# Second routing of a two-layer graph-attention kernel: one more step ahead of the normed row, the row's copy on another engine, later tables, more bias buffers

## The chip, the cores and the metric

The kernel runs on one core of one Trainium2 chip. The metric is device time in microseconds (us), the median of several executions. TensorE is written PE, its weight loads PEld, VectorE DVE, ScalarE ACT, GpSimd POOL; SP is the engine that issues most transfers.

## The reference

Two layers are computed on 2708 rows `x` of 256 numbers. Each layer is a graph attention, then a mixture of eight experts, both added to `x`.

```
x = x + elu(softmax(mask(q k^T / 16)) v)            # first attention, q, k, v of layernorm(x)
x = x + sum over top 2 of w_e * expert0_e(layernorm(layernorm(x)))
x = x + softmax(mask(s_src_i + s_dst_j)) H          # second attention, H = layernorm(x) W + b
x = x + sum over top 2 of p_e * expert1_e(layernorm(x))
```

An expert is two matrix products with a Gelu between them, 256 to 512 to 256 in the second layer. A router (a product with an 8-column matrix) chooses two experts for every row. All is in float32; the mask is an adjacency matrix of integers. The change touches the second layer's routing and experts.

## The kernel before, in words

**Tiles and stages.** The rows are cut into 22 tiles of 128 (the last has 20), numbered 0 to 21. In time the stages are: first attention (to 526 us), first experts (529 to 868), keys and values of the second attention with its first group of tiles (868 to 943), groups 1 to 4 of the second attention (943 to 1056), second experts (1059 to 1265), and the final sum (to the end).

**The second attention** (`layer1_attention`) takes its tiles in groups of 6, 6, 4, 3 and 3 (`GROUPS`). For each group it runs over the 22 blocks of keys, `k`, and in each block multiplies every tile of the group twice (line 713; line 719 for the last block), so that a block of a group of six has 12 matmuls. The sums stay in PSUM and are copied out by `evict` (line 739), which also adds a routing job for each tile to a `Line`.

**The line and its steps.** A routing job is a Python generator, and each `yield` ends a step. `line.step()` advances all jobs that run, oldest first, and starts a waiting one when `line.gap` steps have passed since the last. It is called once for each block of keys in groups of four or six tiles, once for every second block in groups of three, and twice in each slot of the experts. The gap is three steps in groups 1, 3 and 4 and in the slots, and five in group 2. So the tiles of group 0 are routed while group 1 is multiplied, and so on; the last ones are routed beside the first slots of the experts.

**The steps of one tile**, with names used below:

- `z`: the denominators of the softmax (`over_sum`, lines 244 to 249, DVE).
- statistics: the attention is added to `kept` (line 727), the logits are completed (line 730), and `norm_stats` takes mean and variance (lines 209 to 211) and a power -0.5 on POOL (line 215, `ln_rs`).
- row: `normed` makes the row that the experts read (line 219, DVE, needs the power); POOL writes the token number into two rows (line 956) and copies the first row into the second (line 969; DVE does so once `begun` is set).
- `lg`: the gate logits, the two best experts and the selection `sel` (lines 986 to 1007, DVE).
- the exponential of the two best (line 1009, ACT).
- the counting product on PE (lines 1012 and 1013, need `sel` and `seen`).
- `den`: weights and positions (lines 1016 to 1029, DVE), which end with `to`, the row numbers; `seen` is brought up to date (line 1023); then POOL dispatches the two rows into a DRAM table `disp` by indirect transfers (line 1032).

**Early tables.** When 14 tiles are routed (`early`), `begin` starts a generator beside the line: it calls `place` for the first 20 chunks of rows, each of one expert (a product at line 1053 that needs `seen`, then DVE work over lines 1055 to 1144), and then asks for the rows (line 1204, SP) and weights (line 1189, POOL) of the first three chunks.

**The slots of the second experts** (`slots`). A slot s multiplies one chunk of 128 rows: `up` (line 1260, eight pairs of 128x128, Gelu at line 1268), the transposition of the next chunk (line 1237, copied to `xe` at line 1247), a step of the line, `down` of slot s-1 (line 1276), in whose middle slot s+3's weights and rows are fetched, and another step. `down` adds the bias copy `bias2` on DVE (`y`, line 1282), scales it, and POOL stores the rows (line 1287). `bias2` is copied by ACT at the head of `up` (line 1253). Weights lie in a ring of four buffers; a fetch whose chunk has the same expert as the one four slots before moves no data. After slot 8's first step the remaining chunks are placed by a second call of `place`.

**Order.** PE, ACT, DVE and SP take their instructions in the order of the program text here (`manual_schedule`); POOL's order is chosen by the planner. [...]

Of the kernel before, what the change touches and what calls it, by code (L numbers as in the profile page):

```python
# [9 lines left out]
F32 = mybir.dt.float32  # L10
# [10 lines left out]
P = 128  # L21
N = 2708
D = 256
# [39 lines left out]
AHEAD = 3  # L63
# [6 lines left out]
def adj_ffn_kernel(ctx: ExitStack, tc: tile.TileContext, a: dict, out: bass.AP):  # L70
    nc = tc.nc
# [531 lines left out]
    def layer1_attention(mTs, kept, line, first_masks):  # L603
        with ExitStack() as scope:
# [100 lines left out]
            def attend(ts_, k, accs):  # L705
                if k == GROUP:
                    load_tails(ts_)
                masks = next(masks_of_keys) if k < NT - 1 else None
                for t, acc in zip(ts_, accs):
                    r, j = ROWS[t], t % GROUP  # L710
                    if masks:
                        for i in range(2):
                            nc.tensor.matmul(  # L713
                                acc[:r], masks[t], parts[:, k, i],
                                start=(k == 0 and i == 0), stop=False,
                            )
                        continue
                    keys = slice(j * QUARTER, j * QUARTER + TAIL)
                    nc.tensor.matmul(
                        acc[:r, : VALUES + 1], tails[t // GROUP][keys, :r], e_tail[keys], start=False, stop=True  # L720
                    )
# [14 lines left out]
            def evict(ts_, accs, total):  # L736
                for j, (t, acc) in enumerate(zip(ts_, accs)):
                    raw = rows.tile([P, VALUES + 1], F32, name="raw", bufs=6)
                    (nc.scalar.copy if j % 2 else nc.vector.tensor_copy)(  # L739
                        raw[: ROWS[t]], acc[: ROWS[t], : VALUES + 1]  # L740
                    )
                    line.add(finish(t, raw, total))

            def keys_and_values(ts_, accs):

                nc.scalar.activation(spread_of[:, :1], ident[:, :1], AF.Exp)
                def busy(n):  # L750
                    for _ in range(n):
                        nc.tensor.matmul(  # L752
                            accs[0][:, :D], ident, wfc[:, 0, :D], start=True, stop=True
                        )

                busy(PAUSE)
                next(masks_of_keys)
                stats, xn, xT, e = {}, {}, {}, {}
                for i in range(-3, NT + LAG1 - 1):
                    if i + 3 < NT:  # L760
                        stats[i + 3] = norm_begin(i + 3)
                    if 0 <= i - 1 < NT:
                        add_bias(i - 1)
                    if 0 <= i - 1 < NT - 1:
                        second_part(i - 1, e.pop(i - 1))
                    if 0 <= i + 2 < NT:
                        xn[i + 2] = norm_end(i + 2, *stats.pop(i + 2))
                    if 0 <= i + 1 < NT:
                        xT[i + 1] = columns(i + 1, xn.pop(i + 1))
                        if i < 1:  # L770
                            busy(1 - i)
                    if 0 <= i < NT:
                        e[i] = values(i, xT[i])
                    if 0 <= i - 2 < NT:
                        attend(ts_, i - 2, accs)
                    if 0 <= i < NT:
                        nc.vector.tensor_reduce(
                            sums_of[:, :, i], xT.pop(i)[:, :, : ROWS[i]], AX.X, ALU.add
                        )
# [5 lines left out]
            g0, total, beginning = 0, None, None  # L785
            for g, wide in enumerate(GROUPS):
                if g == 2:

                    assert g0 >= FIRST_MASKS * GROUP
                    first_masks.close()  # L790


                    n = FULL_AFTER[experts1.early]
                    guess = experts1.open(
                        [i * (n // RING) * E // (n + GROUP) for i in range(RING)],
                        lambda: converted_last[0],
                    )
                ts_ = list(range(g0, g0 + wide))
                accs = [ps_acc.tile([P, EVEN], F32, name="acc") for _ in ts_]

                every = 2 if wide < GROUP else 1
                line.gap = NT // wide // every
                if g == 0:
                    with tc.manual_schedule(engines={mybir.EngineType.Pool}):
                        keys_and_values(ts_, accs)
                for k in range(NT if g else 0):
                    if g > 0:
                        if g == 2 and k % GROUP == 0:
                            next(guess, None)
                        attend(ts_, k, accs)  # L810
                        if k % every == 0:
                            line.step()
                    if g > 0 and not experts1.begun and experts1.routed >= experts1.early:
                        beginning = experts1.begin()
                    if beginning:
                        next(beginning, None)
                if g == 0:
                    sums = pool.tile([P, DC], F32, name="sums", bufs=1)
                    nc.vector.tensor_reduce(sums, sums_of, AX.X, ALU.add)
                    total = all_sum(pool, sums, wfc, VALUES, "total1")  # L820
                    nc.vector.tensor_add(
                        logits, logits, bfc_gate.unsqueeze(1).to_broadcast([P, NT, E])
                    )
                evict(ts_, accs, total)
                g0 += wide
# [41 lines left out]
    class Experts:  # L867
# [64 lines left out]
        def route(self, t, x, logits=None):  # L932


            own_norm, xd, disp, seen = self.own_norm, self.xd, self.disp, self.seen
            w_gate, gate_bias = self.w_gate, self.gate_bias
            r = ROWS[t]
            rows2 = [
                routing.tile([P, DROW], F32, name=f"row{j}") if own_norm
                else kept_pool.tile([P, DROW], F32, name=f"row{j}", bufs=6)  # L940
                for j in range(2)
            ]
            mean, once, twice, _ = norm_stats(x[:r], r)
            yield
            if own_norm:
                self.beside_early(nc.sync.dma_start(xd[t * P : t * P + r, :], x[:r]))

# [7 lines left out]
            for j in range(2):  # L955
# [4 lines left out]
                if not own_norm:  # L960
# [5 lines left out]
                        ),  # L966
                        reason="no sooner than the row",
                    )
            (nc.vector if own_norm or self.begun else nc.gpsimd).tensor_copy(
                rows2[1][:r, :D], rows2[0][:r, :D]  # L970
            )
            yield
            lg = small.tile([P, E], F32, name="lg")
            if logits is None:
                gT = routing.tile([P, DC, P], F32, name="gT", bufs=2)
# [173 lines left out]
        def begin(self):  # L1149

            assert self.routed >= self.early
            self.begun = True
            return self.begin_steps()

        def begin_steps(self):
            yield from self.place(0, FULL_AFTER[self.early])
            rows_ = [self.fetch_rows(s) for s in range(AHEAD)]
            self.fetched = [(self.fetch_weights(s), rows_[s]) for s in range(AHEAD)]

        def open(self, likely=None, pace=None):  # L1160

# [67 lines left out]
        def slots(self, two, ps_mm, ps_tp, ps_acc, line):  # L1229
            hidden, own_norm, xd = self.hidden, self.own_norm, self.xd  # L1230
# [18 lines left out]

            def up(w, xe):  # L1250

                bias2 = two.tile([P, D], F32, name="bias2")
                (nc.vector.tensor_copy if own_norm else nc.scalar.copy)(bias2, w[:, b2:b1])
                hT = two.tile([P, hc, P], F32, name="hT")
                for g in range(0, hc, GROUP):
                    ps = ps_mm.tile([P, GROUP, P], F32, name="mm")
                    for i in range(GROUP):
                        f = g + i
                        for c in range(DC):
                            nc.tensor.matmul(  # L1260
                                ps[:, i, :],
                                w[:, c * hidden + f * P : c * hidden + (f + 1) * P],
                                xe[:, c, :],
                                start=(c == 0), stop=(c == DC - 1),
                            )
                    for i in range(GROUP):
                        f = g + i
                        nc.scalar.activation(  # L1268
                            hT[:, f, :], ps[:, i, :], AF.Gelu, bias=w[:, b1 + f : b1 + f + 1]
                        )  # L1270
                return hT, bias2
# [103 lines left out]
    experts1 = Experts(1, 512, packed1, wg, gb_b, False, xd1, disps[1], 14)  # L1375
# [79 lines left out]
```

## Time and profile before

| what | us |
|---|---|
| median of 3 runs (lowest, highest) | 1306.93 (1302.76, 1307.99) |
| profiled execution, its own time | 1296.54 |
| its span, first to last instruction | 1294.8 |
| PE busy | 1204.9 |
| DVE busy | 552.4 |
| ACT busy | 439.1 |
| POOL busy | 424.3 |

Durations come from the profiled execution alone. In a line of the timeline the first number is the start in us from the span's start, the second the duration, and a bracket gives the idle time of the engine before it and what ended it. "issue" there means that the profile shows no releaser. Line numbers are those of the kernel before.

### The profile page before, as it was taken

To read this page: it belongs to the slowest core of one execution; us is meant where nothing else is said; L and a number is where in the kernel's file an instruction comes from. 1 tells how busy PE (TensorE), PEld (TensorE's weight loads), DVE (VectorE), ACT (ScalarE), POOL (GpSimd) and SP (SyncE) were. 2 spreads that over 40 slices of the span, in tenths; PEclk is the share of its full clock that TensorE was granted. 3 is DMA by queue.
4 is the path that set the end of the run, shared out by engine and by line. 5 is a ranking of instruction groups with operands and counts; after the bars stand their busy time and mean duration, and the time that the engine had idled before them with its cause. 6 is when DMAs were issued, how large, how long until landed. Compare 5 with 4: busy or idle time off the path is not lost. (4 is left out here: it accounts for less than half of the span.)

```text
span 1294.8 us, 20983 instructions
## 1 busy us (share of the span) xinstructions
PE 1204.9 (93%) x7136; PEld 972.2 (75%) x7136; DVE 552.4 (43%) x2087; ACT 439.1 (34%) x1286; POOL 424.3 (33%) x553
## 2 busy tenths in 40 slices
PE   7999999999999999999999999999998768899990
PEld 4776666656566675799999999988998757799880
DVE  6623833634625526542212121217767766311114
ACT  3221212212122212433232323325765447444440
POOL 4100110110110113243333333335645557555450
PEclk9999999999999999899999999999999979999995
DMA  8601364996946715356657745432005115544357
GB/s 268 223 1 66 107 179 124 255 239 175 261 112 159 168 62 231 143 170 171 212 160 243 281 121 173 110 99 85 1 26 189 42 58 180 174 137 145 119 180 261
DMA packets 107242, 197.83 MB, mean 153 GB/s; under 512 B 26753, under 2 KB 81718, under 8 KB 100986
## 3 DMA queue, kind: packets, MB, share of 16 engines
q1 hardware_dynamic: 77276, 110.09, 29.8%
q0 software_dynamic: 27040, 83.56, 20.4%
q10 hardware_dynamic: 2814, 2.77, 0.7%
q8 instruction: 59, 0.97, 0.3%
q14 instruction: 53, 0.43, 0.1%
HBM read 263.63 MB, written 66.12 MB: 255 GB/s over the span
## 5 line engine op out<-in xcount | busy, mean ns | idle before, releaser
L1260 PEld LDWEIGHTS mm<-xe,ring 128*128 128x128 f32 x2192 | 268.5, 196 | 28.9 <-ACT xe L1247 15.0
L1260 PE MATMUL mm<-xe,ring 128*128 128x128 f32 x2192 | 277.7, 281 | 12.2 <-ACT xe L1247 8.7
L1276 PE MATMUL acc<-ring,hT 128*128 128x256 f32 x1096 | 267.4, 382 | 3.0 <-ACT hT L1268 3.0
L1268 ACT ACTIVATE hT<-mm,ring 128x128 f32<-128x128 f32 x548 | 156.1, 368 | 255.7 <-issue 181.6
L1276 PEld LDWEIGHTS acc<-ring,hT 128*128 128x128 f32 x1096 | 195.3, 191 | 23.2 <-ACT hT L1268 3.6
L504 PE MATMUL acc<-v,p 128*128 128x257 f32 (+1 forms) x880 | 209.7, 390 | 0.0
L447 PE MATMUL s<-g,xnT 128*128 128x512 f32 x420 | 205.6, 604 | 4.1 <-DVE mT L459 4.1
L1282 DVE TENSOR_TENSOR y<-acc,bias 128x256 f32<-128x256 f32 x92 | 39.0, 424 | 368.5 <-PE acc L1276 365.6
L504 PEld LDWEIGHTS acc<-v,p 128*128 128x128 f32 (+1 forms) x880 | 153.7, 191 | 18.3 <-issue 0.8
L1189 POOL DMA_INDIRECT ring<-L_ffn_packed,weight_row x98 | 102.9, 1050 | 195.4 <-issue 153.2
L1032 POOL DMA_INDIRECT disp<-row,to x88 | 88.1, 1001 | 145.7 <-DVE to L1029 57.8
L215 POOL TENSOR_TENSOR ln_rs<-ln_rs,minus_half 128x2 f32<-128x2 f32 x88 | 66.4, 755 | 200.7 <-DVE ln_rs L211 183.4
L713 PE MATMUL acc<-parts,m 128*128 128x266 f32 x924 | 129.2, 297 | 1.8 <-DVE raw L739 1.1
L459 DVE TENSOR_SCALAR mT<-s 128x512 fp8e4<-128x512 f32 x105 | 72.0, 686 | 130.4 <-ACT p L458 130.3
L713 PEld LDWEIGHTS acc<-parts,m 128*128 128x128 f32 x924 | 119.5, 190 | 9.2 <-issue 3.3
L458 ACT ACTIVATE p<-s 128x512 f32<-128x512 f32 x105 | 62.3, 594 | 165.3 <-PE s L453 165.1
L447 PEld LDWEIGHTS s<-g,xnT 128*128 128x128 f32 x420 | 75.1, 191 | 50.1 <-issue 41.6
L1294 POOL DMA_INDIRECT xd<-y,xg x45 | 70.9, 1577 | 80.4 <-issue 36.4
L453 PEld LDWEIGHTS <-apart 128*128 128x128 fp8e4 x420 | 32.7, 99 | 61.2 <-issue 61.2
L685 ACT CAST m<-mT 128x512 fp32r<-128x512 fp8e4 (+4 forms) x168 | 70.6, 473 | 14.1 <-PE acc L713 11.8
L334 DVE TENSOR_SCALAR apart<-adj 128x677 fp8e4<-128x677 int32 x80 | 40.9, 514 | 53.3 <-DMA adj<-in_adj_dram 52.7
L1287 POOL DMA_INDIRECT xd<-y,xg x47 | 47.3, 1006 | 21.1 <-PE tp L1237 8.5
(227 smaller groups left out, 1158.6 us busy)
## 6 DMA issues: line engine op xcount, KB each, us to landing
adj<-in_adj_dram SPq DMA_DIRECT2D x84, 338.5 KB
L_ffn_packed<-in_L_ffn_W_dram SPq DMA_DIRECT2D x16, 1024.0 KB
xg<-disp SPq DMA_DIRECT2D x98, 129.0 KB
L_ffn_packed<-in_L_ffn_W_dram SPq DMA_DIRECT2D x16, 512.0 KB
neighbours<-mT SPq DMA_DIRECT2D x5, 1408.0 KB
mT<-neighbours SPq DMA_DIRECT2D x5, 1408.0 KB
xin<-in_x_dram SPq DMA_DIRECT2D x42, 128.0 KB
ring<-L_ffn_packed SPq DMA_DIRECT2D x4, 1154.0 KB
```

The source lines that it names most:

```text
L215: nc.gpsimd.tensor_tensor(rs[:r, 1], rs[:r, 0], minus_half[:r], ALU.pow)
L447: nc.tensor.matmul(ps[:kr, :nb], xnT[:, c, k0 : k0 + kr], g[:, c, :nb], start=(c == 0), stop=False,)
L459: nc.vector.tensor_scalar(mT[:kr, k, :], ps[:kr, :nb], -BIG / 2, None, ALU.is_gt, saturate=False,)
L504: nc.tensor.matmul(accs[j][:r], p[keys, q0 : q0 + r], v[keys, k, :], start=(k == 0), stop=(k == NT - 1),)
L685: nc.scalar.copy(m[:, : q1 - q0], mTs[b][:, k, q0 - b * BN : q1 - b * BN])
L713: nc.tensor.matmul(acc[:r], masks[t], parts[:, k, i], start=(k == 0 and i == 0), stop=False,)
L1032: nc.gpsimd.indirect_dma_start(disp[:], bass.IndirectOffsetOnAxis(ap=to[:r, j : j + 1], axis=0), rows2[j][:r], None,)
L1189: nc.gpsimd.indirect_dma_start(w, None, packed[:], bass.IndirectOffsetOnAxis(ap=self.weight_row[:, s : s + 1], axis=0), bounds_check=E * P ...
L1260: nc.tensor.matmul(ps[:, i, :], w[:, c * hidden + f * P : c * hidden + (f + 1) * P], xe[:, c, :], start=(c == 0), stop=(c == DC - 1),)
L1268: nc.scalar.activation(hT[:, f, :], ps[:, i, :], AF.Gelu, bias=w[:, b1 + f : b1 + f + 1])
L1276: nc.tensor.matmul(ps, hT[:, f, :], w[:, w2 + f * D : w2 + (f + 1) * D], start=(f == 0), stop=(f == hc - 1),)
L1294: start = nc.gpsimd.indirect_dma_start(xd[:], at, y, None, bounds_check=N - 1, oob_is_err=False, compute_op=ALU.add)
```

## The change

It has four parts, all in the second layer. A tile's routing gets an empty step between its statistics and its normed row. The copy of the first row into the second moves one step later and from POOL to ACT (to DVE, as before, once `begun` is set). The generator that `begin` returns has one more step ahead of it, sets `begun` only then, and asks for one chunk's weights in a step, where it asked for three in one. The bias copy in the slots has four buffers, where it had two. The first layer takes the same code with `own_norm` set: its row and its bias are as they were, and its generator of early tables is run through at one place.

```diff
-                    if g > 0 and not experts1.begun and experts1.routed >= experts1.early:
+                    if g > 0 and not beginning and experts1.routed >= experts1.early:
                         beginning = experts1.begin()
...
             mean, once, twice, _ = norm_stats(x[:r], r)
             yield
+            if not own_norm:
+
+                yield
...
-            (nc.vector if own_norm or self.begun else nc.gpsimd).tensor_copy(
-                rows2[1][:r, :D], rows2[0][:r, :D]
-            )
+            if own_norm:
+                nc.vector.tensor_copy(rows2[1][:r, :D], rows2[0][:r, :D])
             yield
+            if not own_norm:
+                (nc.vector.tensor_copy if self.begun else nc.scalar.copy)(
+                    rows2[1][:r, :D], rows2[0][:r, :D]
+                )
             lg = small.tile([P, E], F32, name="lg")
...
         def begin(self):
 
             assert self.routed >= self.early
+            return self.begin_steps()
+
+        def begin_steps(self):
+            yield
             self.begun = True
-            return self.begin_steps()
-
-        def begin_steps(self):
             yield from self.place(0, FULL_AFTER[self.early])
             rows_ = [self.fetch_rows(s) for s in range(AHEAD)]
-            self.fetched = [(self.fetch_weights(s), rows_[s]) for s in range(AHEAD)]
+            self.fetched = []
+            for s in range(AHEAD):
+                self.fetched.append((self.fetch_weights(s), rows_[s]))
+                yield
...
-                bias2 = two.tile([P, D], F32, name="bias2")
+                bias2 = two.tile([P, D], F32, name="bias2", bufs=2 if own_norm else 4)
```

More of the change, by code (lines that the diff above doesn't have):

```diff
@@ L1151, in begin @@
             assert self.routed >= self.early
-            self.begun = True
             return self.begin_steps()
         def begin_steps(self):
+            yield
+            self.begun = True
             yield from self.place(0, FULL_AFTER[self.early])
             rows_ = [self.fetch_rows(s) for s in range(AHEAD)]
-            self.fetched = [(self.fetch_weights(s), rows_[s]) for s in range(AHEAD)]
+            self.fetched = []
+            for s in range(AHEAD):
+                self.fetched.append((self.fetch_weights(s), rows_[s]))
+                yield
         def open(self, likely=None, pace=None):
```

## The prediction

> **What bounds the kernel now.** I read the busy times by stage first, then the waits of the second routing, then the timeline of VectorE and GpSimd around one tile. Only 944 to 1130 us is touched: all edited lines but the generator of `begin` ask for `not own_norm`, and in the first experts that generator is run through at once. The stages are groups 1 to 4 of the second attention and the first twelve slots of the second experts. The columns are PE, PEld, DVE, ACT and POOL busy with counts, the granted clock, DMA share and GB/s:
>
> ```profile
> 945.20:978.70 33.50, 32.31 (x266) 31.80 (x266) 26.28 (x140) 19.32 (x52) 17.11 (x33) 1.00 0.09 33
> 980.00:1007.60 27.60, 22.55 (x185) 21.80 (x185) 17.62 (x96) 13.11 (x36) 14.22 (x29) 1.00 0.61 218
> 1007.60:1027.80 20.20, 19.01 (x141) 18.02 (x138) 15.06 (x79) 10.40 (x32) 10.79 (x19) 0.92 0.10 35
> 1027.80:1059.50 31.70, 20.03 (x144) 16.91 (x141) 24.54 (x133) 11.59 (x50) 18.92 (x29) 0.90 0.21 63
> 1059.50:1072.00 12.50, 10.73 (x49) 9.74 (x50) 3.57 (x18) 7.92 (x18) 2.33 (x6) 0.58 0.07 22
> ```
>
> The reader is to see PE almost full in group 1 (first row) and then losing ground: 5 of 27.6 us in group 2, and 11.7 of 31.7 in group 4 with the wait for its eviction (fourth row). The fifth row, slots 0 and 1, runs at clock 0.58. The waits of the routing (line, releaser, total us, times, longest) name what is late:
>
> ```profile
> DVE row L219 <- POOL ln_rs L215: 29.1, 21, 3.5
> ...
> ACT bias L1253 <- DVE y L1282: 10.6, 5, 4.3
> ```
>
> Line 219 is the normed row; it sits in VectorE's queue and waits for GpSimd's power. One tile of group 3, in the timeline of all engines:
>
> ```profile
> 1022.53 0.41 DVE L219 TENSOR_SCALAR row<-kept,ln_mv,ln_rs 128x256 f32<-128x256 f32 x1 [0.84 <-POOL ln_rs L215]
> ...
> 1023.78 0.17 DVE L1029 TENSOR_REDUCE to<-hot 128x2 int32<-128x16 f32 x1
> ...
> 1027.38 0.72 POOL L215 TENSOR_TENSOR ln_rs<-ln_rs,minus_half 128x2 f32<-128x2 f32 x1 [0.18 <-DVE ln_rs L211]
> ...
> 1028.13 0.41 DVE L219 TENSOR_SCALAR row<-kept,ln_mv,ln_rs 128x256 f32<-128x256 f32 x1 [0.84 <-POOL ln_rs L215]
> ```
>
> From row to row is 5.60 us: 4.76 of VectorE work and 0.84 in which VectorE stands at the row for the power. The work by its starts in this timeline: row 0.33, `den` to `to` 1.01 (1.09 until `to` is ready), `lg` to `sel` 1.02 (1.11 until ready), `z` 0.97, statistics 1.43. Twelve attention matmuls a step (36 a tile, 0.129 us each) give PE 4.64 us a tile, so PE is released by VectorE (`sel`, line 1007) here. In group 2 the loop is longer:
>
> ```profile
> 987.00 0.17 DVE L1029 TENSOR_REDUCE to<-hot 128x2 int32<-128x16 f32 x1
> ...
> 987.95 1.04 POOL L1032 DMA_INDIRECT disp<-row,to  x1 [2.88 <-issue]
> ...
> 991.07 0.41 DVE L219 TENSOR_SCALAR row<-kept,ln_mv,ln_rs 128x256 f32<-128x256 f32 x1 [2.56 <-POOL ln_rs L215]
> ```
>
> `to` (ready at 987.17) releases the two dispatches at 987.95; only behind them does GpSimd take the next tile's power (990.29), and the row comes 3.9 us after `to`. PE needs 5.2 us a tile there, the loop takes 7.1 (row at 991.07, next at 998.18). At the end of group 4:
>
> ```profile
> 1054.80 0.17 PE L1012 MATMUL misc<-sel,before 128*128 128x8 bf16 x1 [3.52 <-DVE sel L1007]
> ...
> 1059.61 0.66 PE L1237 MATMUL tp<-ident,xg 128*128 128x128 f32 x2 [3.43 <-issue]
> ```
>
> PE waits 3.5 us for a row stalled behind GpSimd, and 3.4 for the last accumulators, whose VectorE copy (1058.76 to 1059.51) stands behind the same queue.
>
> [...] The trace agrees: it grants half clock for 3.4 us from 1008.5 and from 1035.8, and for 13.7 us from 1056.3, four such pieces, each after a stretch of these waits. [...]
>
> **The change, part by part.**
>
> *One step more ahead of the row.* A tile takes eight steps for seven. In group 2 a tile starts each fifth step. Before, the next tile's statistics were issued just behind `to` in the same step, so its power queued behind the two dispatches. Now they are issued a step ahead of `to`, the power goes ahead of the dispatches, and the row comes two steps (2.1 us) after the statistics. The loop becomes PE's own 5.2 us; the waits 1.22, 1.88 and 1.88 go: 5.0 us. Late next is PE itself.
>
> In groups 1, 3 and 4 a tile starts each third step, and there the step separates nothing: the added step is one in which VectorE has nothing else, so the row still follows its statistics directly. Worse, `z` of the next tile (0.97 us) now lies between row and `to`, and the power stays behind the dispatches. The new loop is row to `to` 0.33 + 0.97 + 1.09 = 2.39, `to` to dispatch 0.79, two dispatches 2.33, power and row 0.77: **6.28 us** a tile for 5.60. In group 1 the tiles 2 to 5 pay it; the first two have no dispatches ahead. With tile 1's row at 953.6, tile 2's comes 6.65 later at 960.3 and tile 4's at 972.8; its `sel` is 0.33 + 0.97 + 1.01 + 1.11 later, 976.3. PE is there at 974.7, waits, and ends group 1 at 976.3 + 4.64 + 1.1 = 982.1 for 979.8: 2.3 us lost. Group 2 then costs 176 matmuls x 0.1295 + 1.0 = 23.8: it ends at 1005.9 for 1007.6. Group 3 takes 132 x 0.129 = 17.0, plus 0.9 for its last wait and the tails: 1023.8 for 1027.8. The half clock at 1008.5 (1.7 us) should go with group 2's waits. In group 4 PE needs 17.6 us, and VectorE is behind: the rows of tiles 12 and 13 come at 1019.2 and 1025.5; `sel` of 13 is 0.33 + 0.97 + 0.77 (eviction) + 1.01 + 1.11 later, 1029.7, and PE is there at 1027.7: 2.0. Tile 14's row is 3.89 after tile 12's `to`, 1032.6, tile 13's `seen` 2.0 later and 0.2 more to PE; PE comes to line 1053 at 1032.1: 2.7. Then VectorE has one `lg`, one statistics, the whole table and the next `den` and `lg`, 10.9 us, until tile 15's `sel` at 1045.5; PE is there at 1041.8: 3.7. Two statistics, a row with its stall, `z`, `den`, a copy, `lg` and the eviction, 8.5 us, end at 1054.0; PE is there at 1050.3: 3.7. So the eviction ends 30 us after 1023.8, for 31.7: slots begin about 1053.8 for 1059.6, **6 us** earlier.
>
> *Row copy by ScalarE.* Fifteen 0.39 us copies (line 969) leave GpSimd, whose wait hides them in the loop above, so no gain. ScalarE takes 0.41 for one (its 128x256 copy, line 1253) with 14 us idle in the 33.5 of group 1: no cost while the row is ready a step before; its cover is the row's lead of 3.4 us over `sel`. Queued behind it are the mask casts, made two steps of keys ahead. If it were late, the second dispatch waits for it (rival D).
>
> *Early tables a step later, one gather per step.* Three gathers (1.05 us each, line 1189), three row loads on SP, the table's VectorE chain of about 4.6 us: none added. The placing matmul now comes a step of keys behind `seen` (0.8 us): its wait of 2.91 at line 1053 stays at the 2.7 above because VectorE is late itself. The row loads go out at about 1043 and land in 2.2 to 8.8 us; slots begin at 1054. The gathers no longer stand together ahead of a dispatch (3 x 1.35 us at 1044.9 to 1048.9 before the tile-14 pair): tile 16's power is 2.7 us earlier, counted above.
>
> *Four bias buffers.* ScalarE's copy of the bias waits for the `y` of two slots before, which releases its buffer, and Gelu and `xe` are behind it:
>
> ```profile
> 1109.66 0.40 ACT L1253 COPY bias<-ring 128x256 f32<-128x256 f32 x1 [4.31 <-DVE y L1282]
> ```
>
> By this the next matmuls came 1.78 us late. Other such waits in slots 2 to 10: 0.73, 1.60, and 0.9 of one of 2.69; with the 1.8, 5.0 can go. But GpSimd is full there (26.6 busy of 33.75, the rest mostly 0.3 us pieces between DMAs), and real gathers of weights were issued at 1079.1, 1084.5 and 1087.8. In the new order slot 7's comes behind 3 gathers (1.35), 3 stores (1.32), 4 dispatches (1.3), 2 powers (0.9) and 2 index pairs (0.45): 15.9, plus 0.9 to its start and 6.7 to land: 23.5 us after slot 0's down product, for 24.9. Behind slot 9 the 1.8 go. **3 us**, between 0 and 5.0. Slots 0 and 1 I leave at half clock[...].
>
> Sum: 6 + 3 = **9 us**. The profiled execution took 1296.54 (span 1294.8), 0.8% under the median 1306.93; the saving is in the same stages, so I take it off the median: 1298.
>
> **The rivals.** About 0.5% (6.5 us) is what a measurement here can tell from no change. *A, above:* 1298, own range 1291 to 1304. *B, the waits vanish.* If the power no longer stands behind the dispatches in groups 3 and 4, VectorE's 4.76 us a tile is left: 10 tiles x 1.5 = 15 us beyond A's groups at most, of which PE can use about 8, and a clock kept full in slots 0 and 1 gives 5: 1306.9 - 22 = 1285. For it: GpSimd was 10.8 of 20.2 us busy in group 3. Against: [...]the order in them puts the dispatches first. *C, given back.* The clock stays half for two windows more, 2 x 1.7 us, and the slots stay tied to GpSimd's chain of 34 us from slot 0: 9 - 3.4 - 3 = 3 us, 1304. *D, slower.* ScalarE's row copy comes later than 0.79 + 1.34 = 2.1 us after `to`, behind casts that wait for PE, and holds the second dispatch, so the loop of 6.28 grows. At 7.2 us over the 10 tiles of groups with a gap of three the 9 us are gone; at 8 it is 10 x 1.7 - 9 = 8 us slower, 1315. Against: the row is ready a step before. That the change does nothing: if all loops stayed as they are, 1307; the instruction order moved, so only part of C.
>
> **How the numbers follow.** A 0.57 (0.49 of it beyond 6.5 us), B 0.14, C 0.17, D 0.12. Faster 0.63, same 0.25, slower 0.12. The range 1286 to 1309 leaves out D and the far end of B.
>
> **What would show it.** In the timeline after: rows 6.3 us apart in groups 1 and 3, 5.2 in group 2; group 2 without waits for `sel`; line 1053 still waiting over 2 us; slots begun 5 to 7 us earlier; no wait of the bias for `y`. Rows 5.6 or fewer us apart in group 3 make my loop wrong; a second dispatch long after the first makes D right; slots beginning no earlier make the sum wrong.

## The result, and the profile after

The change made the kernel faster. In the comparison beside the kernel before, four runs each, it took 1290.99 us (1287.64 to 1294.16) against 1305.96 (1302.76 to 1307.99): a ratio of 0.9881, with a 95% interval of 0.985 to 0.9912. Measured twice more as a base of the experiments, the same kernel gave 0.9903 [0.9876, 0.9931] and 0.9928 [0.9901, 0.9954]. The mean of the three is 0.990, so about 12 us of 1300 are gained, where 9 were forecast; the first comparison shows 15. The profiled execution took 1287.64 us (span 1285.9), against 1296.54 (1294.8) before. Of these 9 us, 4.5 lie ahead of the second routing (the copy of `total` that opens it comes at 939.59 for 944.10), in instructions that the change leaves alone, so spans are not compared below. What is compared is the stretch from that copy on.

The stages first, in the same columns as before (start and end, length, PE, PEld, DVE, ACT and POOL busy with counts, clock, DMA share, GB/s): groups 1 to 4 and the first slots of the kernel after. Its lines stand lower by the lines added above them: `sel` is line 1013 (1007 before), `to` 1035 (1029), the dispatch 1038 (1032), the table's product 1059 (1053), the transposition 1247 (1237), Gelu 1278 (1268).

```profile
940.70:975.60 34.90, 33.30 (x272) 32.37 (x273) 24.67 (x134) 21.00 (x56) 14.39 (x30) 1.00 0.09 31
975.60:1000.50 24.90, 23.76 (x184) 23.05 (x184) 21.09 (x114) 15.12 (x43) 14.43 (x23) 0.93 0.72 241
1000.50:1017.40 16.90, 16.90 (x145) 16.36 (x141) 13.36 (x74) 11.52 (x35) 8.65 (x15) 1.00 0.11 38
1017.40:1046.40 29.00, 21.66 (x142) 17.78 (x139) 22.91 (x123) 11.87 (x52) 16.56 (x25) 0.86 0.24 70
1046.40:1058.90 12.50, 10.91 (x69) 10.10 (x70) 6.37 (x33) 6.96 (x19) 5.79 (x8) 0.77 0.10 33
```

Against the rows of before, PE is no longer losing ground in group 2 (23.76 of 24.90 us, where it had 22.55 of 27.60) and is never idle in group 3 (16.90 of 16.90). The clock of group 2 is 0.93, for 1.00: a piece of half clock of 3.4 us fell at its start. Group 4 still has 7.3 us of idle PE, for 11.7. The slots start with less half clock: 0.77 for 0.58.

The waits of the same stretch say the same of VectorE (line, releaser, total us, times, longest). PE's wait for a selection before:

```profile
PE misc L1012 <- DVE sel L1007: 12.2, 10, 3.5
```

And the waits after:

```profile
DVE row L219 <- POOL ln_rs L215: 19.8, 15, 2.0
...
PE misc L1018 <- DVE sel L1013: 3.6, 4, 1.4
...
PE misc L1018 <- DVE hot L1006: 1.8, 1, 1.8
```

The row's wait for its power has 15 cases for 21 and a longest of 2.0 us for 3.5, but it is not gone. PE's waits for a selection fall from 12.2 us to 5.4: the 3.6 of the second line, and 1.8 for the selection of tile 15, which stands under `hot`, an earlier step of the same work. The bias copy's wait for `y`, 10.6 us before, has no line any more.

Group 2 in the timeline of all engines (start, us, engine, line, operation; a bracket gives the idle time before and what ended it):

```profile
990.76 0.22 DVE L211 SCALAR_TENSOR_TENSOR ln_rs<-once_twice,ln_mv 128x2 f32<-128x2 f32 x1
...
991.07 0.72 POOL L215 TENSOR_TENSOR ln_rs<-ln_rs,minus_half 128x2 f32<-128x2 f32 x1 [0.32 <-DVE den L1022]
...
991.75 0.17 DVE L1035 TENSOR_REDUCE to<-hot 128x2 int32<-128x16 f32 x1
992.03 0.41 DVE L219 TENSOR_SCALAR row<-kept,ln_mv,ln_rs 128x256 f32<-128x256 f32 x1
...
992.70 1.04 POOL L1038 DMA_INDIRECT disp<-row,to  x1 [0.91 <-POOL ln_rs L215]
...
994.04 1.12 POOL L1038 DMA_INDIRECT disp<-row,to  x1 [0.30 <-issue]
...
996.63 0.41 DVE L219 TENSOR_SCALAR row<-kept,ln_mv,ln_rs 128x256 f32<-128x256 f32 x1
```

Statistics of the next tile (line 211) now come ahead of `to`, so the power (991.07) stands ahead of the two dispatches (992.70, 994.04), and the row at 992.03 carries no bracket. The next row comes at 996.63, 4.6 us later.

One tile of group 3:

```profile
1012.96 0.41 DVE L219 TENSOR_SCALAR row<-kept,ln_mv,ln_rs 128x256 f32<-128x256 f32 x1 [1.54 <-POOL ln_rs L215]
...
1014.98 0.17 DVE L1035 TENSOR_REDUCE to<-hot 128x2 int32<-128x16 f32 x1
...
1015.93 1.04 POOL L1038 DMA_INDIRECT disp<-row,to  x1 [2.19 <-issue]
...
1017.28 0.98 POOL L1038 DMA_INDIRECT disp<-row,to  x1 [0.30 <-issue]
...
1018.28 0.73 POOL L215 TENSOR_TENSOR ln_rs<-ln_rs,minus_half 128x2 f32<-128x2 f32 x1
1019.04 0.41 DVE L219 TENSOR_SCALAR row<-kept,ln_mv,ln_rs 128x256 f32<-128x256 f32 x1 [1.52 <-POOL ln_rs L215]
```

`to` at 1014.98 releases the dispatches at 1015.93 and 1017.28, the power comes behind them at 1018.28, and the next row stands 1.52 us, where before it stood 0.84. Work that did not need the row stood with it: the sums of the next tile lay copied out since 1001.4 (line 739), and VectorE, idle for 1.54 us at the row of 1012.96, began that tile's `z` behind the row, at 1013.29. From row to row is 6.1 us.

The places where PE still waits late in group 4, and the first transposition of the slots:

```profile
1022.98 0.17 PE L1018 MATMUL misc<-sel,before 128*128 128x8 bf16 x1 [1.10 <-DVE sel L1013]
...
1027.71 0.17 PE L1059 MATMUL misc<-seen,ones 128*128 128x8 bf16 x1 [1.92 <-DVE seen L1029]
...
1038.04 0.17 PE L1018 MATMUL misc<-sel,before 128*128 128x8 bf16 x1 [1.75 <-DVE hot L1006]
...
1046.45 0.66 PE L1247 MATMUL tp<-ident,xg 128*128 128x128 f32 x2 [2.23 <-issue]
```

The selection of tile 13, `seen` in front of the early table, tile 15's selection and the last eviction (the bracket names no releaser for it, before either) cost PE 1.10, 1.92, 1.75 and 2.23 us, 7.0 in all.

The stretch up to the slots repeats to 0.1 us in three profiles of the kernel after, so it serves as the ruler for the experiments. It runs from `total` to the eviction of each group (line 739 on DVE) and then to the first transposition (line 1247, 1237 before); each column is the step from one to the next in us, each row one profile.

| kernel | group 1 | group 2 | group 3 | group 4 | to the slot | sum |
|---|---|---|---|---|---|---|
| before | 35.40 | 30.25 | 21.76 | 27.25 | 0.85 | 115.5 |
| after | 36.76 | 24.25 | 19.62 | 25.37 | 0.86 | 106.9 |
| after, second profile | 36.75 | 24.24 | 19.61 | 25.37 | 0.86 | 106.8 |
| after, third profile | 36.75 | 24.24 | 19.62 | 25.39 | 0.86 | 106.9 |
| step alone | 37.27 | 23.75 | 20.39 | 29.19 | 0.86 | 111.5 |
| copy alone | 35.02 | 30.25 | 21.62 | 25.99 | 1.06 | 113.9 |
| tables alone | 35.46 | 31.51 | 21.80 | 27.12 | 0.86 | 116.7 |
| bias alone | 35.40 | 31.51 | 21.79 | 27.35 | 0.86 | 116.9 |
| all but the step | 34.99 | 30.26 | 21.60 | 25.71 | 1.06 | 113.6 |
| all but the copy | 37.25 | 23.77 | 20.38 | 26.44 | 0.85 | 108.7 |
| all but the tables | 36.78 | 23.97 | 19.64 | 28.01 | 0.86 | 109.3 |
| all but the bias | 36.75 | 23.97 | 19.61 | 25.36 | 0.86 | 106.6 |
| two steps more | 33.74 | 24.34 | 15.55 | 22.70 | 0.86 | 97.2 |
| two steps more, second profile | 33.72 | 24.36 | 15.53 | 22.66 | 1.01 | 97.3 |

The 31.51 of group 2 in two rows is not of these two parts' making: up to there every engine runs the same instructions in the same order as before. In both the clock was half for 3.4 us twice, at the start of the group (980.1 and 976.8 us) and again later (1000.6 and 997.3): 48 matmuls of line 713 took 7.68 us in both at the start, and later 40 took 6.71 and 6.70, for 5.19 at full clock. Before, the clock was full until 1008.5. One profile of such a stage is thus good to about 1.3 us. In all, 8.65 us are gained by the time that the slots begin.

### The profile page after: what moved, and what is told of

Same layout as the page of the kernel before. It is cut to its first block, busy times and chain, and to the rows that moved or that the text cites. A ratio compares the mean times of both kernels' runs of the same rounds, so it can differ in the third digit from the quotient of the medians.

```text
span 1285.9 us, 20986 instructions
## 1 busy us (share of the span) xinstructions
PE 1200.1 (93%) x7136; PEld 967.9 (75%) x7136; DVE 551.0 (43%) x2087; ACT 439.9 (34%) x1301; POOL 420.2 (33%) x538
## 5 line engine op out<-in xcount | busy, mean ns | idle before, releaser
L1270 PE MATMUL mm<-xe,ring 128*128 128x128 f32 x2192 | 274.4, 279 | 17.7 <-ACT xe L1257 12.6
L1270 PEld LDWEIGHTS mm<-xe,ring 128*128 128x128 f32 x2192 | 264.9, 194 | 33.1 <-ACT xe L1257 14.9
L1297 POOL DMA_INDIRECT xd<-y,xg x47 | 47.3, 1007 | 24.8 <-PE tp L1247 9.1
```

Of the source, the lines that this page charges most:

```text
L1270: nc.tensor.matmul(ps[:, i, :], w[:, c * hidden + f * P : c * hidden + (f + 1) * P], xe[:, c, :], start=(c == 0), stop=(c == DC - 1),)
```

## The experiments

In each group the kernels ran beside the kernel before on one chip. In that order its medians were 1291.65, 1295.89 and 1298.02 us, so only ratios are carried from one group to the next.

### The four parts, each alone

The **step** alone is the kernel before with only

```diff
             yield
+            if not own_norm:
+
+                yield
             if own_norm:
```

> The kernel before with the empty step alone; the row copy stays on GpSimd, the tables and the bias buffers as before. Theory (order of power and dispatches): group 2's rows come 5.2 us apart for 7.1 and its three waits of PE for sel go (5.0 us); in groups 1 and 3 the rows come about 6.1 to 6.3 us apart for 5.6, since the power stays behind the dispatches and z now lies between row and to. Together 4 to 7 us faster than before. Rival (it is the copy that held GpSimd): with the copy still on GpSimd nothing is gained, 0 or up to 3 us slower.

Measured: 1286.13 us, ratio 0.9948 [0.9931, 0.9965], by which it is about 7 us faster by itself. Group 2 shrinks to 23.75 us, with rows 4.6 to 4.9 apart, and group 1 loses 1.9. But the gain is partly given back in group 4 (29.19 for 27.25). Its timeline:

```profile
1039.29 1.11 POOL L1192 DMA_INDIRECT ring<-L_ffn_packed,weight_row  x1 [2.01 <-ACT m L685]
...
1040.70 1.17 POOL L1192 DMA_INDIRECT ring<-L_ffn_packed,weight_row  x1 [0.30 <-ACT p L1012]
...
1041.71 0.22 DVE L211 SCALAR_TENSOR_TENSOR ln_rs<-once_twice,ln_mv 128x2 f32<-128x2 f32 x1
1042.17 0.99 POOL L1192 DMA_INDIRECT ring<-L_ffn_packed,weight_row  x1 [0.30 <-ACT m L685]
1043.46 1.02 POOL L1035 DMA_INDIRECT disp<-row,to  x1 [0.30 <-issue]
...
1044.79 1.00 POOL L1035 DMA_INDIRECT disp<-row,to  x1 [0.31 <-issue]
1045.82 0.74 POOL L215 TENSOR_TENSOR ln_rs<-ln_rs,minus_half 128x2 f32<-128x2 f32 x1
1046.59 0.47 DVE L219 TENSOR_SCALAR row<-kept,ln_mv,ln_rs 128x256 f32<-128x256 f32 x1 [4.66 <-POOL ln_rs L215]
...
1052.30 0.66 PE L1240 MATMUL tp<-ident,xg 128*128 128x128 f32 x2 [6.92 <-issue]
```

Three gathers of weights and two dispatches stand in POOL's queue ahead of a power that was ready at 1041.93: VectorE stands 4.66 us at the row, and PE waits 6.92 us for the first transposition. So the early table's three gathers cost time there. They are not all of the 1.9 us that group 4 lost: its clock was half for 10.2 us from 1025.6, where before it was half for 3.4 us from 1035.8.

The **row copy** alone moves line 969 from POOL to ACT and one step later, as in the diff above.

> The kernel before with the row copy alone moved to ScalarE, a step later. Theory: rows stay 5.6 us apart in groups 1 and 3 and 7.1 in group 2, because GpSimd waited for to anyway; 0, within 2 us. Rival (GpSimd's 0.39 us a tile are on the path): rows 5.2 us apart in groups 1 and 3, about 4 to 5 us faster.

Measured: 1288.87 us, ratio 0.9984 [0.9969, 0.9999], about 2 us, at the edge of what can be told. The rows come 5.5 us apart for 5.6 in groups 1 and 3 and stay 7.1 apart in group 2; group 4 is 1.3 us shorter.

The **tables** alone are the later `begun` and one gather in a step.

> The kernel before with the early tables a step later and one gather a step, alone. Theory: the placing matmul waits some 0.8 us less for seen (2.1 for 2.91), and the power behind three gathers and two dispatches (a stall of 3.5 us at the row) comes 2 to 3 us earlier: 1 to 3 us faster. Rival (later fetches are late): the first slot waits for its rows or weights, 0 to 3 us slower.

Measured: 1292.68 us, ratio 0.9998 [0.9983, 1.0013]: nothing. PE waits 2.19 us for `seen` where it had 2.91, and 3.40 for the selection of a later tile.

The **bias buffers** alone:

```diff
-                bias2 = two.tile([P, D], F32, name="bias2")
+                bias2 = two.tile([P, D], F32, name="bias2", bufs=2 if own_norm else 4)
```

> The kernel before with four bias buffers alone. Theory: ScalarE no longer waits for y; the 1.8 us after slot 9 and part of three smaller waits go: 3 us faster, between 0 and 5. Rival (GpSimd's chain of gathers, stores and dispatches sets the pace of slots 2 to 10): the waits of ScalarE go and PE waits for weights or for xe in their place, 0.

Measured: 1291.32 us, ratio 0.9998 [0.9986, 1.001]: nothing. The wait of 1.78 us behind slot 9 is gone, but PE meets the next ones, for weights and rows that have not landed. Its timeline on PE:

```profile
1114.80 2.02 PE L1260 MATMUL mm<-xe,ring 128*128 128x128 f32 x16 [1.90 <-DMA ring<-L_ffn_packed,weight_row]
1118.23 0.41 PE L1237 MATMUL tp<-ident,xg 128*128 128x128 f32 x2 [1.41 <-DMA xg<-disp]
```

Before, the longest wait for gathered weights was 1.1 us. The other profile with four buffers and without the step, all but the step (below), has the same two waits, 1.60 for weights and 2.01 for rows, while the copy alone and the tables alone, with two buffers, keep the wait of 1.78 us (1.78 and 1.75). So the slots were held by two things one behind the other, and only the nearer one was taken away.

### The whole change, and all but one part

**The whole change once more**, as the base of this group:

> The changed kernel once more, as the base of the three beside it. Theory: 13 to 17 us faster than before, as measured. Groups 1 and 3 with rows 6.1 us apart. The pause of 5.6 us in ScalarE and VectorE near 1090 us of its first profile should not come again if it was an accident of that execution; if it belongs to the program it comes at the same instructions.

Measured: 1282.89 us, ratio 0.9903 [0.9876, 0.9931]. Each stage up to the slots is within 0.02 us of the first profile.

**All but the step** (the three added lines left out):

> The changed kernel without the empty step. Theory (the step is the largest part): 5 to 8 us slower than the changed kernel, with group 2's waits for sel back at 1.2 to 1.9 us each. Rival (copy, tables and bias carry the gain): within 2 us of the changed kernel.

Measured: 1293.01 us, ratio 0.998 [0.9962, 0.9998]. The stretch to the slots is 113.6 us: 6.8 of the 8.65 go with the step.

**All but the bias buffers** (`bufs=2` again):

> The changed kernel with two bias buffers again. Theory: 3 us slower than the changed kernel, up to 6, since with VectorE free of the stall at the row y is nearer in time but the copy of the bias still waits for it behind the second table. Rival (GpSimd sets the pace of the slots): within 1 us.

Measured: 1283.94 us, ratio 0.9912 [0.9884, 0.9941], 1 us over the whole change of the same group, which the intervals don't separate. This and the run of the bias alone agree that these buffers bring nothing that can be measured here. The trace has another reason for it than that of the bias alone: with the step there is no long wait left to take away. Up to 1125 us the bias copy waits for `y` 1.0 us at most here, and at most 1.0 in the step alone, both with two buffers; before, and with the copy or the tables alone, its longest wait is 4.3.

In the last group, with the whole change beside them, came the two parts that were left. **All but the tables**:

> The change without its tables part (extra step, ScalarE row copy and four bias buffers stay; the early table is begun with its placing and all three gathers of one step, as before). Theory 1, the step and the tables need each other: as with the step alone, three gathers and two dispatches stand ahead of the power of a late tile in group 4, its row stalls 4 to 5 us near 1045 us, the first transposition of the slots waits 6 to 7 us and the slots begin 4 to 5 us later than with the whole change; the time is 0.992 to 0.995 of the kernel before. Theory 2, the tables part is worth nothing, as the tables alone were: the late row stalls no more than 1.5 us, the first transposition waits about 2 us, and the ratio is that of the whole change, about 0.990.

Measured: 1289.81 us, ratio 0.993 [0.9902, 0.9958], beside 0.9928 for the whole change: the times do not tell them apart. The trace does:

```profile
1046.12 0.47 DVE L219 TENSOR_SCALAR row<-kept,ln_mv,ln_rs 128x256 f32<-128x256 f32 x1 [3.92 <-issue]
...
1051.74 0.66 PE L1243 MATMUL tp<-ident,xg 128*128 128x128 f32 x2 [6.16 <-issue]
```

The late row stands 3.92 us for 1.33, the first transposition waits 6.16 for 2.23, and the slots begin 2.4 us later (109.3 for 106.9). The order in the queue is the one that the first theory said, and the row and PE wait as long as it said; at the slots, half of its price is left.

**All but the copy** (the row copy on POOL again):

> The change with the row copy left on GpSimd (step, tables and bias stay). Theory 1, the copy lies beside other work: rows of groups 1 and 3 again 6.1 us apart, group 2 without waits for sel, the slots begin within 1 us of those of the whole change, ratio about 0.990. Theory 2, fifteen copies of 0.39 us on GpSimd lengthen the loop from row to row through GpSimd: rows of groups 1 and 3 6.5 us apart, 2 to 3 us later at the slots, ratio about 0.992.

Measured: 1293.06 us, ratio 0.9951 [0.9933, 0.997]. The rows of groups 1 and 3 are 6.2 us apart for 6.1, and the slots begin 1.8 us later. By the times the copy is worth more, 1293.06 against 1288.35, but the intervals of the two overlap. Both the ruler and the times speak for the second theory. Where the 0.1 us of a tile lie can be read in the timeline of this kernel:

```profile
1013.56 0.39 POOL L972 COPY row<-row 128x256 f32<-128x256 f32 x1
1013.63 0.62 DVE L249 SCALAR_TENSOR_TENSOR raw<-total,z,raw 128x264 f32<-128x264 f32 x1
```

and at the same place in that of after:

```profile
1013.75 0.47 DVE L249 SCALAR_TENSOR_TENSOR raw<-total,z,raw 128x264 f32<-128x264 f32 x1
```

`z` scales the sums (line 249, from `total` and `raw`). While POOL copies the row, this takes 0.62 us for 0.47: nine of its 21 cases in this profile lie beside such a copy and take 611 to 620 ns, the other twelve 473 to 477. What makes it longer was not shown. Without the step it is another instruction that lies beside the copy and is longer: before, the update of `seen` (line 1023) takes 0.28 to 0.29 us for 0.15 in nine tiles, all of groups 1, 3 and 4, and not in group 2, where the copy alone left the rows 7.1 us apart. So the copy on POOL cost VectorE 0.13 to 0.15 us a tile there, also where POOL had time to spare.

**The whole change, third time**:

> The whole change once more, as the base of the others of this call. The earlier call gave 0.9903 [0.9876, 0.9931] of the kernel before. If the gain is the second routing and its end, rows, waits and the first transposition repeat to within 1 us of the earlier profile and the ratio is 0.988 to 0.993; if part of it was chance of executions, the ratio falls to 0.993 or above (the 9 us forecast would be 0.993).

Measured: 1288.35 us, ratio 0.9928 [0.9901, 0.9954]. The stages repeat to 0.04 us, so the routing's share is steady; what varies from one comparison to the next lies elsewhere.

### Two steps more instead of one

If groups with a gap of three lose because the step separates nothing there, a second step should put the power ahead of the dispatches in them too:

```diff
             if not own_norm:
-
+                yield
                 yield
```

> The changed kernel with two empty steps for one. In groups with a gap of three the statistics of the next tile now come a step ahead of to, as in group 2, so the power goes ahead of the dispatches. Theory: rows 4.8 us apart in groups 1 and 3 for 6.1, the waits of PE for sel at the end of group 1 go (2.5 us), those of group 4 shrink: 3 to 7 us faster than the changed kernel. Rival (VectorE's own work, 4.76 us a tile and the tables, is what PE waits for in group 4, and a later route delays the end): within 2 us, or slower by up to 3.

Measured: 1276.83 us, ratio 0.9861 [0.9833, 0.9889], beside 0.9903 for the whole change in the same group. It was run again:

> The change with two steps more ahead of the row instead of one, once more. If the power ahead of both dispatches in groups 1, 3 and 4 is worth 5 us, as the earlier call suggested (1276.8 beside 1282.9), this is 3 to 7 us faster than the whole change of this call, rows of groups 1 and 3 about 4.7 us apart without a stall. If the earlier difference was chance, it is within 2 us of the whole change.

Measured: 1282.87 us, ratio 0.9882 [0.9842, 0.9923], beside 0.9928. Both times it is 5 to 6 us faster than the change, and it beats both kernels. The intervals of the two overlap a little each time; the ruler sets them apart. Group 3 in its timeline:

```profile
1008.55 0.41 DVE L219 TENSOR_SCALAR row<-kept,ln_mv,ln_rs 128x256 f32<-128x256 f32 x1
...
1010.10 0.22 DVE L211 SCALAR_TENSOR_TENSOR ln_rs<-once_twice,ln_mv 128x2 f32<-128x2 f32 x1
...
1010.40 0.72 POOL L215 TENSOR_TENSOR ln_rs<-ln_rs,minus_half 128x2 f32<-128x2 f32 x1 [0.21 <-DVE den L1022]
...
1011.08 0.17 DVE L1035 TENSOR_REDUCE to<-hot 128x2 int32<-128x16 f32 x1
...
1012.03 1.05 POOL L1038 DMA_INDIRECT disp<-row,to  x1 [0.91 <-ACT m L685]
...
1013.39 0.97 POOL L1038 DMA_INDIRECT disp<-row,to  x1 [0.31 <-issue]
...
1014.28 0.41 DVE L219 TENSOR_SCALAR row<-kept,ln_mv,ln_rs 128x256 f32<-128x256 f32 x1
```

The power at 1010.40 is taken ahead of the dispatches at 1012.03 and 1013.39, and the rows carry no bracket. Rows are 3.6 to 5.7 us apart in group 3, PE waits for no selection up to tile 15, and the stretch to the slots is 97.2 us, 9.6 less than after. By the times, some 4 of these are lost again behind it. In the first profile PE waits twice for weights in the slots, 2.07 and 2.05 us, and in both ACT loads its function tables 13 times from the first transposition on, for 11 in every other kernel (1.28 us each); which of this costs the time was not separated.

### What was not settled

After, the third profile and three others of kernels that have both the step and four bias buffers show ACT and DVE standing still for 3.5 to 7 us in the slots, with half clock for 6.8 us from about the end of it. The timeline of after, and of the second profile at the same instructions:

```profile
1095.45 1.28 ACT L1278 ACT_TABLE_LOAD   x1 [6.73 <-remote]
1095.48 0.17 DVE L1061 COPY n_e<-misc 128x8 f32<-128x8 f32 x1 [5.60 <-remote]
```

```profile
1088.60 1.28 ACT L1278 ACT_TABLE_LOAD   x1 [0.54 <-PE mm L1270]
...
1088.81 0.17 DVE L1061 COPY n_e<-misc 128x8 f32<-128x8 f32 x1
```

"remote" means that no instruction of the core is seen to release them; in the second profile the same two instructions go at once. It came in five of the seven profiles with both parts and in none of the other seven. The whole change took 239.5 and 234.9 us from the first transposition to the end with it, and 226.4 without; before took 235.2. Over all fourteen profiles this stretch is 234.9 to 244.8 us with the pause and 226.4 to 236.3 without. It may thus take back what the slots could gain, and be why the three comparisons of one kernel differ. What releases ACT and DVE there, and whether the pairing is more than chance, is open.

## Why the prediction was right, and where it was not

**Faster, and why: right.** The step carries it. All but the step leaves 2 of 12 us, the step alone brings 7. The mechanism in group 2 is the one forecast: the power goes ahead of the dispatches, and the waits 1.22, 1.88 and 1.88 are gone. Its loop was put at PE's own 5.2 us and is 4.6 to 4.8.

**The loop in groups 1 and 3: right.** 6.28 us a tile were forecast for 5.60, and rows are 6.1 apart, with the stall that follows from the order of POOL's queue (1.54 for 0.84). This is the counterpart of the usual hope: the added step made these tiles slower, and it still paid. Two steps more confirm the cause, since with the power ahead of the dispatches the stall is nil.

**What it costs group 1: right in sign, too large.** 2.3 us were forecast to its end. By PE's last matmul of the group it is 0.3, and 0.9 more for tile 5's selection, which fell behind the group's end instead of ahead of it; by the eviction it is 1.4.

**The sum of the routing: mis-sized, 6 us for 8.65.** The forecast gave group 3 a last wait of 0.9 us, and none came. In group 4 it summed waits of 2.0, 2.7, 3.7 and 3.7, 12.1 in all, where the profile has 1.10, 1.92, 1.75 and 2.23, 7.0. Of that, PE gains only 1 us, since the 29.0 us of group 4 hold two pieces of half clock that the forecast left out. With the copy on POOL the four waits are 2.18, 0.79, 3.57 and 1.78, and the slots begin 6.8 us earlier than before: so two thirds of the 2.65 us that were missing are the copy, which the forecast took at nothing.

**Row copy: the term that failed there.** Its cover was said to be GpSimd's own wait. That holds for POOL, but not for VectorE beside it, which is the engine that sets the loop. It brings 1.6 us of the ruler alone and 1.8 in the whole. Rival D is not seen in any run: no second dispatch waited for ACT's copy. Nor was a function table loaded on ACT for the copy: the loads from 900 us on, 1.28 us each, are 11 before and after.

**Early tables: right, as part of the sum.** The forecast had the gathers no longer ahead of a dispatch, so that a late power comes 2.7 us earlier. Its row's stall is 2.6 us shorter than without this part (1.33 for 3.92), and the slots begin 2.4 us earlier. Alone the part is worth nothing (0.9998), and "none added" held: with the step it matters because the step brings the table, its gathers and the dispatches together in one stretch of POOL's queue.

**Bias buffers: wrong, 3 us for nothing.** The wait was seen rightly and it does go. The step that failed is the one behind it, where weights were said to be 1.4 us in time: without the routing step PE waits 1.60 to 1.90 us for them there. And the 3 us were added to the 6 of the routing, though with the step the long wait is gone with two buffers too (1.0 us at most for 4.3), so they were counted for what another part does; how the step does it was not followed. The low end of its own bounds, 0, is what came.

**Half clock in the slots: not as forecast.** It was left at 13.7 us and is 6.8 in each profile of the whole change, an estimated 3.4 us of PE's time at half speed. But the tables and the bias alone, which begin their slots as late as before, had 10.2 and 6.8 us, so how much of this is the change's doing is open. The piece at 1008.5 is gone, as forecast, but one at 977.1 came for it, behind the new waits at the end of group 1; all but the tables and all but the bias, with the same instructions there, do not have it.

So of 12 us, 8.65 are the routing (2.65 more than forecast) and none the buffers (3 fewer). The 3 or so that are left no run places. Less half clock at the start of the slots would cover them, but what varies there anyway is larger: 226.4 to 239.5 us from the first transposition to the end in three profiles of one kernel. That the total came near the forecast is in part luck, since the routing was put too low and the buffers too high by about the same.

## What to carry to other kernels

An instruction that stands behind others in its engine's queue (before, in group 2, the power could start at 988.51 and started behind the two dispatches, at 990.29) was moved by changing what is issued ahead of it, and the count of steps that this took went with the gap between jobs: one step was enough at a gap of five, two were needed at three. Cost each part of a change on the kernel that has the other parts in it: the tables were worth nothing alone and 2.4 us beside the step, and a copy that one engine had time for still slowed its neighbour (0.62 us for 0.47). Before a buffer wait is counted as a gain, find what would be late next behind it, and whether another part of the change takes it away already: here the weights took its place without the step, and with the step it was gone.

## What the runs showed of the hardware

Half clock came here behind stretches in which PE was working. From group 1 to the first slots of the kernel after it came in pieces of 3.4 us, once of twice that, each behind a stretch of 3.4 us in which PE was busy for 1.48 to 2.31 us. Windows of the kernel after, each the 3.4 us ahead of a piece of half clock, in the columns of the stages:

```profile
973.70:977.10 3.40, 2.25 (x22) 1.67 (x21) 2.85 (x18) 1.83 (x7) 1.66 (x8) 0.99 0.12 41
1024.90:1028.30 3.40, 1.48 (x13) 1.24 (x12) 2.32 (x14) 1.37 (x6) 1.15 (x4) 0.99 0.11 39
1035.10:1038.50 3.40, 1.60 (x13) 1.23 (x12) 3.16 (x24) 0.76 (x5) 2.04 (x2) 1.00 0.31 75
1041.90:1045.30 3.40, 2.31 (x15) 1.18 (x13) 3.19 (x20) 0.57 (x3) 2.57 (x5) 1.00 0.17 33
```

And one that kept the full clock behind it:

```profile
1021.40:1024.80 3.40, 2.25 (x18) 1.73 (x18) 2.67 (x17) 2.12 (x12) 1.80 (x2) 1.00 0.12 41
```

PE was busy 2.25, 1.48, 1.60 and 2.31 us of 3.40 in the first four, up to two thirds of the stretch. Before, too, where the prediction has each piece after a stretch of waits, PE was busy for 1.73 us of the 3.40 ahead of the piece at 1008.5. Busy time alone did not decide here, since the fifth stretch has the same 2.25 us as the first; what did is open.

In the profiles of before and after the pieces start whole multiples of 3.413 us from one another (before: 1008.50, 1035.80, 1056.28; after: 977.05, 1028.25, 1038.49, 1045.32). Why the same instructions of group 2 were hit in some profiles and not in others was not shown.
